# Late storing of the scales, another bank for fillers, and loads of h without pacing in a cross-attention and FFN kernel

## The chip, the cores and the metric

The kernel runs on one core of a Trainium2 chip. The metric is device time in microseconds (us), lower is better. A core has a matrix engine (TensorE, PE in the profile), a vector engine (VectorE, DVE), an activation engine (ScalarE, ACT), a general engine (GpSimd, POOL) and a queue engine (SyncE, SP); each works through its own list of instructions in order and waits on semaphores for the others. DMA transfers are issued here by SP and by POOL, and 16 DMA engines carry them all. PE writes its results to PSUM, 8 banks on chip; SBUF is the large memory on chip, DRAM the one off chip.

## The reference

Input x has 8 x 1024 rows of 512 columns, ctx 8 x 64 rows. In float32:

```python
x = x + xattn(layernorm(x), ctx)      # 16 heads of 64, softmax with a clip at +-11
z = layernorm(x)
# FFN with fake quantisation to 8 bits; scale = sigmoid(clip) * max|.| / 127 over ALL elements
xq = act_fake_quant(z, clip_x)
gate = xq @ weight_fake_quant(w_gate).T    # 512 -> 1408, a scale per output row of the weight
up   = xq @ weight_fake_quant(w_up).T
h = act_fake_quant(silu(gate) * up, clip_down)
out = x + h @ weight_fake_quant(w_down).T  # 1408 -> 512
```

Two maxima over everything cut the work into three: z is quantised only when its last row is known, and h only when the last element of silu(gate)*up is known. These two places are called the first and the second seam.

## The kernel before

The 8192 rows are 64 tiles of 128. **Attention** (0 to 786 us in the profile) runs over the tiles and stores x after attention to DRAM as `x1_d`; in its spare time it also quantises the weights and stores them to DRAM. The scale of each of the 512 rows of w_down ends in the tile `swd` (128 partitions x 4). The kernel writes `swd` to a small DRAM tensor `swd_d` (lines 921 to 923: 512 elements, each its own place in DRAM), so that it can later be loaded broadcast to all partitions as `sdb` (line 1058).

**Gate and up** (791 to 1099 us; lines 993 to 1042) run over 16 groups `g` of 4 tiles (512 rows), and within a group over 11 blocks `i` of 128 features. Per block there are 8 matmuls of 128x512, a Silu on ACT, a product on VectorE, and for every second block a maximum over the pair. A pair of blocks (`j`, 88 in all, 512 KB each in float32) is the unit in which h is kept. PE's results alternate between two buffers `g` (gate) and two buffers `u` (up), one bank each, of the PSUM pool `ps2`. While group g is computed, the rows of group g+1 are made ready: SP loads them from `x1_d` into `xi` (issued at i = 8 two groups ahead; three buffers), VectorE quantises them (`x8`, at i = 2, 3, 5, 6), ACT copies them to bfloat16 (`xb`, one buffer for two tiles, at i = 3, 4, 6, 7), and SP transposes them by DMA into `xT` (`xT<-xb`, two transpositions a group, at i = 4 and i = 7). The first matmul of group g+1 needs both transpositions.

44 pairs (groups 0 to 7) go out to DRAM (`h_d`) as they are made; the other 44 stay on chip: 37 in the pool `hp`, two in PSUM (`pk`), the last five in room of the gate and up weights that is no longer needed.

**The second seam** (lines 1043 to 1058). `keep_clock` issues matmuls whose result nobody reads, so that PE is not idle: 8 before and 5 after the matmul `amh`, through which `all_max` spreads the maximum over all partitions. They write to `kcq`, half of a two-bank buffer `o` of the new PSUM pool `ps3`, which lies where `ps2` was. The matmul `amh` stands behind the first 8 in PE's list.

**The down projection** (1104 to 1259 us; lines 1060 to 1170) takes the pairs in the order `todo`: first the resident ones, then the 44 that are loaded back. `quant_to` quantises pairs some way ahead of PE (ACT to int8, VectorE or every sixth time ACT to bfloat16 `hb`). `load_h` issues the loads `hr<-h_d` on POOL's queue as the count of quantised pairs rises: up to `LD0 + (nld - LD0) * 2 * done / (LDG * 11)` loads, and no more than buffers have come free (`room`). Ahead of each load POOL copies one element of the `hb` of the pair two back into `pace`, so the load goes out no earlier than that pair has been cast. `hp` is shared: from `HBL` pairs before the end the `hb` take its buffers too. `finish` scales the result on VectorE (`wguT<-o,wguT`; the output buffers are also in the old weights' room, hence the name), adds x (`wguT<-wguT,x1r`), stores the output and issues the next load `x1r` on SP's queue (three buffers). For the last group the addition left from the group before is given to POOL (`E=G`). The x of the last group comes by POOL's queue as the last two loads (`hr<-x_d`).

In VectorE's list the casts for later pairs stand behind the `finish` of earlier tiles, and in SP's list each `x1r` behind an output store. All of it is in the order in which the program is written: each call is kept in program order on its engine.

Of the kernel before, what the change touches and what calls it, by code (L numbers as in the profile page):

```python
# [8 lines left out]
F32 = mybir.dt.float32  # L9
F16 = mybir.dt.float16  # L10
BF = mybir.dt.bfloat16
# [3 lines left out]
ALU = mybir.AluOpType  # L15
# [12 lines left out]
KC0 = 12  # L28
KC1 = (2, 7)
KC2 = (8, 5)  # L30
LD0 = 8
LDG = 15
HBL = 33
CAST = 6
XB = 5
# [31 lines left out]
def kernel(  # L67
# [16 lines left out]
    nc = tc.nc  # L84
    V, S, G, T, D = (_InOrder(tc, e) for e in (nc.vector, nc.scalar, nc.gpsimd, nc.tensor, nc.sync))
    P = 128
    NT, DM = x.shape
    NTILE = NT // P
    NGRP = NTILE // 4
# [16 lines left out]
    dram = pool("scratch", space=DRAM)  # L106
# [35 lines left out]
    swd = cst.tile([P, NC], F32, name="swd")  # L142
# [49 lines left out]
    for i in range(4):  # L192
        t = p1.tile([P, DM], F32, tag="x", bufs=XB, name=f"ctxn{i}")
# [13 lines left out]
    for j in range(8):  # L207
        if j == 4:
            for i in range(2):
                c = slice(i * 512, (i + 1) * 512)  # L210
                D.dma_start(out=Wv_s[:, :, c], in_=wkv_v[:, :, 1024:2048][:, :, c])
        r = slice(2 * j % 8, 2 * j % 8 + 2)
        t = p1.tile([P, 2, DM], F32, tag=("e", "ph")[j // 2], bufs=2, name=f"wst{j}") if j < 4 else wof[:, r]
# [435 lines left out]
    FW = {}  # L649
# [78 lines left out]
    def load_x1(g):  # L728
        for t in range(4 * g, 4 * g + 4, 2):
            xi = FW["px"].tile([P, 2, DM], F32, tag="xi", bufs=NXI, name=f"xi{t}")  # L730
            D.dma_start(out=xi, in_=x1_d[t // 2])
            xi_t[t], xi_t[t + 1] = xi[:, 0], xi[:, 1]
# [161 lines left out]
    ps2 = pool("ps2", space=PSUM, es=es2)  # L894
    hp = pool("hp", side="left")

    def keep_clock(q, n, w):

        for _ in range(n):
            T.matmul(q, lhsT=w[:, 0, :], rhs=w, start=True, stop=True)  # L900
# [11 lines left out]
    kcq = ps2.tile([P, 4, P], F32, tag="g", bufs=2, name="kcq").rearrange("p i t -> p (i t)")  # L912
# [4 lines left out]
    keep_clock(kcq, KC1[1], FW["gu"][:, 0, 0])  # L917
    V.reciprocal(gq[:, 1:2], gq[:, 9:10])


    swd_d = dram.tile([DM], F32, tag="swd_d", name="swd_d")
    with nc.allow_non_contiguous_dma(reason="512 scales"):
        D.dma_start(out=swd_d.rearrange("(o p) -> p o", p=P), in_=swd)

    hmx = FW["hmx"]
    x8_t, xb_t = {}, {}

# [56 lines left out]
    x1t = {}  # L984
# [10 lines left out]
    for g in range(NGRP):  # L995
        xT = xTs.pop(g)
        for i in range(NF):
            if g == 0 and i == 0:
                load_x1(1)
            if i == 9 and 0 < g <= NC:  # L1000
                w_trans(5 + g)
            if i == 8 and g + 2 < NGRP:
                load_x1(g + 2)
            k = g * NF + i
            j = k // 2
            h = h_tile(j)[:, k % 2]
            sl = h_tile(JX)[:, 1] if JX - NPK <= j < JX else h
            qs = [ps2.tile([P, 4, P], F32, tag="gu"[w], bufs=2, name=f"q{g}_{i}_{w}") for w in range(2)]
            if k == 0:
                xT = xq_first(qs)  # L1010
            else:
                for w in range(2 if k < NK - 1 else 1):
                    for c in range(NC):
                        T.matmul(qs[w], lhsT=FW["gu"][:, i, w, c, :], rhs=xT[:, :, c, :],
                                 start=(c == 0), stop=(c == NC - 1))
            qs = [q.rearrange("p i t -> p (i t)") for q in qs]
            S.activation(sl, qs[0], AF.Silu, scale=swg[:, 0, i : i + 1])
            if g + 1 < NGRP and i - 1 in XQ:
                xq_b(4 * g + 4 + XQ.index(i - 1))
            if k == NK - 1:  # L1020

                ql = [qs[1], ps2.tile([P, 4, P], F32, tag="g", bufs=2, name="q_half").rearrange("p i t -> p (i t)")]
                for hf in range(2):
                    r = slice(hf * 256, (hf + 1) * 256)
                    for c in range(NC):
                        T.matmul(ql[hf][:, r], lhsT=FW["gu"][:, i, 1, c, :], rhs=xT[:, 2 * hf : 2 * hf + 2, c, :],
                                 start=(c == 0), stop=(c == NC - 1))
                    V.scalar_tensor_tensor(h[:, r], ql[hf][:, r], swg[:, 1, i : i + 1], sl[:, r], ALU.mult, ALU.mult)
                    V.tensor_reduce(hmx[:, j + 2 + hf : j + 3 + hf], h[:, r], AX.X, ALU.max, apply_absolute_value=True)
            else:  # L1030
                V.scalar_tensor_tensor(h, qs[1], swg[:, 1, i : i + 1], sl, ALU.mult, ALU.mult)
                if k >= NK - 4:
                    n = k - NK + NPAIR + 2
                    V.tensor_reduce(hmx[:, n : n + 1], h, AX.X, ALU.max, apply_absolute_value=True)
                elif k % 2:
                    V.tensor_reduce(hmx[:, j : j + 1], h_p[j], AX.XY, ALU.max, apply_absolute_value=True)
            if g + 1 < NGRP and i in XQ:
                xq_a(4 * g + 4 + XQ.index(i))
            if g == NGRP - 1 and i < NXI:
                load_r()  # L1040
            if k % 2 and j < NSP:
                D.dma_start(out=h_d[j], in_=h_p.pop(j))
    es2.close()


    p3 = pool("p3", side="right")
    ps3 = pool("ps3", space=PSUM)
    amh = ps3.tile([P, P], F32, tag="o", bufs=2, name="amh")
    kcq = ps3.tile([P, 2, 512], F32, tag="o", bufs=2, name="kcq")[:, 1]
    keep_clock(kcq, KC2[0], FW["d"][:, :, 0])  # L1050
    V.tensor_reduce(gq[:, 4:5], hmx, AX.X, ALU.max)

    all_max(gq[:, 2:3], gq[:, 4:5], amh,
# [5 lines left out]
    hb_t = {}  # L1059
# [8 lines left out]
    nlo = len(loads)  # L1068
    done = 0
    hbx = None  # L1070
    pace = p3.tile([P, 1], BF, name="pace")

    def load_h(k):

        while loads and nlo - len(loads) < k:
            n = nlo - len(loads)
            j = loads.pop(0)

            G.tensor_copy(pace, hb_t[done - 2][:, 0, 0:1])
            h = w_room(2 * n - 2, 2) if n in (4, 5) else hp.tile([P, 2, 512], F32, tag="h", bufs=NHP, name=f"hr{n}")  # L1080
            if j < 0:
                x1t[-1 - j] = h
                G.dma_start(out=h, in_=x1_d[(-1 - j) // 2])
            else:
                h_p[j] = h
                G.dma_start(out=h, in_=h_d[j])
# [29 lines left out]
            hb_t[done] = hb  # L1116
            done += 1

    def finish(q, t, n, c=slice(0, DM), E=V):

        nonlocal o_n
        o = o_q[o_n % 3][:, t % 2 : t % 2 + n, c]
        V.tensor_tensor(o, q, sdb[:, c].unsqueeze(1).to_broadcast([P, n, c.stop - c.start]), ALU.mult)
        E.tensor_tensor(o, o, x1t[t - t % 2][:, t % 2 : t % 2 + n, c], ALU.add)
        D.dma_start(out=out_v[t // 2][:, t % 2 : t % 2 + n, c], in_=o)
        if (t + n) % 2 == 0 and c.stop == DM:
            o_n += 1
            x1t.pop(t + n - 2)
            load_r()
# [8 lines left out]
    for n, g in enumerate(order):  # L1138
        last = n == NGRP - 1
        q = []  # L1140
        for i in range(4 if last else 2):
            pl, tg = (pk, "hk") if n % 2 and i < 2 else (ps3, "o")
            q.append(pl.tile([P, 2, 4, P], F32, tag=tg, bufs=2, name=f"o{g}_{i}").rearrange("p i c t -> p i (c t)"))
        if last:
            q = [t[:, 0:1] for t in q]
        cuts = (0, NF) if last else (0, 3, 5, 7, 9, 11) if n % 2 else (0, 2, 4, 6, 8, 11)
        for f0, f1 in zip(cuts[:-1], cuts[1:]):
            for i in range(4):

                halves = [slice(0, DM)] if not last or i < 3 else [slice(0, DM // 2), slice(DM // 2, DM)]  # L1150
                for c in halves:
                    o = q[i][:, 0, c] if last else q[i // 2][:, i % 2]
                    if last and c.start:
                        o = pk.tile([P, 2, 512], F32, tag="hk", bufs=NPK, name="o_half")[:, 0, c]
                    for f in range(f0, f1):
                        k = n * NF + f
                        T.matmul(o, lhsT=hb_t[k // 2][:, k % 2, i * P : (i + 1) * P],
                                 rhs=FW["d"][:, c.start // P : c.stop // P, f, :], start=(f == 0), stop=(f == NF - 1))
                    if i == 0:
                        quant_to(-(-(n * NF + f1) // 2) + max(2, n + 8 - NGRP))  # L1160
                        load_h(min(LD0 + (nld - LD0) * 2 * done // (LDG * NF), room()))
                    while ends and (last or i % 2 == 0):
                        finish(*ends.pop(0), E=G if last else V)
                        if not last:
                            break
                    if f1 == NF:
                        if last:
                            finish(o.unsqueeze(1), 4 * g + i, 1, c)
                        elif i % 2:
                            ends.append((q[i // 2], 4 * g + i - 1, 2))  # L1170
# [40 lines left out]
```

## Time and profile before

| what | value |
|---|---|
| time, median of 3 runs | 1267.13 us (1266.77 to 1267.4) |
| the profiled execution's own time | 1267.21 us |
| its span | 1265.1 us |
| PE busy | 1243.3 us, 98% |
| VectorE busy | 1027.1 us, 81% |
| ACT busy | 672.4 us, 53% |
| POOL busy | 336.0 us, 27% |
| loads of h, `hr<-h_d` | 42 of 512 KB, median 7.2 us from issue to landing |
| loads `x1r<-x_d` | 30 of 512 KB, median 6.9 us |
| output stores | 30 of 512 KB, median 5.1 us |
| store `swd_d<-swd` | 1 of 2 KB, 10.4 us |
| transpositions `xT<-xb` | 30, median 3.1 us |

How to read it: the page gives busy times by engine and, in 40 slices of the span, the busy share in tenths, the granted clock of PE (PEclk; 9 stands for 90% or more) and the busy share of the DMA engines. A line of a window gives start and end, the length, the busy time (and number of instructions) of PE, weight loads, DVE, ACT and POOL, the granted clock, the DMA share and GB/s. A line of the timeline gives start, duration, engine, line, operation, output<-inputs, shapes and count, and in brackets how long the engine had been idle before it and who ended that. Nearly all instructions carry line 59, that of the helper that records them, so one goes by the names of the tiles. The duration of a matmul of 128x512 in the rows (0.38 us) contains its way through the array; the next one starts 0.216 us after it.

### The profile page before, as it was taken

How to read it: one execution, taken by the hardware profiler on the slowest of the kernel's cores; microseconds unless marked ns; L12 is line 12 of the kernel's file. 1: busy time of each engine (PE TensorE's matmuls, PEld its weight loads, DVE VectorE, ACT ScalarE, POOL GpSimd, SP SyncE). 2: the span in 40 equal slices, each digit the busy share in tenths (PEclk: the TensorE clock that was granted, in tenths of full speed). 3: DMA queues.
4: the chain of work that ended last, by engine and by line, in shares of the span. 5: the costliest groups of instructions: out<-in, count | busy, mean ns of one | idle time of the engine just before them, and what ended most of it. 6: DMA issues, size and time to landing. Idle time of an engine off the chain costs nothing. (4 is left out here: it accounts for less than half of the span.)

```text
span 1265.1 us, 19838 instructions
## 1 busy us (share of the span) xinstructions
PE 1243.3 (98%) x7395; PEld 570.7 (45%) x7395; DVE 1027.1 (81%) x1663; ACT 672.4 (53%) x855; POOL 336.0 (27%) x411
## 2 busy tenths in 40 slices
PE   8999999999999999999999999999999999999997
PEld 4444444444444444444444445444444444444443
DVE  6998788888888888877777767788888888787787
ACT  6765455555555544445555433455455454467673
POOL 2224433343433443334343342000000000042221
PEclk9999999999999999999999999999999999999999
DMA  9238677787777876668776797778873332299997
GB/s 354 55 70 173 130 153 176 184 173 173 170 179 182 174 158 161 161 165 177 170 171 166 164 191 136 197 242 250 260 214 104 92 100 59 67 330 418 386 346 265
DMA packets 322049, 236.99 MB, mean 187 GB/s; under 512 B 258081, under 2 KB 263713, under 8 KB 321953
## 3 DMA queue, kind: packets, MB, share of 16 engines
q1 hardware_dynamic: 315328, 211.61, 64.7%
q0 software_dynamic: 6624, 24.12, 5.1%
q8 instruction: 58, 0.95, 0.3%
q14 instruction: 39, 0.31, 0.1%
HBM read 112.21 MB, written 60.95 MB: 137 GB/s over the span
## 5 line engine op out<-in xcount | busy, mean ns | idle before, releaser
L59 PE MATMUL sc<-M,lat 128*128 128x512 f16 x1536 | 341.8, 379 | 1.5 <-DMA lat<-lh 1.5
L59 PE MATMUL pv<-N,PT 128*128 128x512 f16 (+1 forms) x1560 | 342.2, 376 | 0.4 <-DVE x L59 0.2
L59 PE MATMUL q<-xT,wguT 128*128 128x512 bf16 x1408 | 304.6, 379 | 2.8 <-DVE h L59 1.6
L59 POOL TENSOR_TENSOR ph<-e,ph 128x1024 f16<-128x1024 f32 x62 | 132.1, 2131 | 401.9 <-ACT ph L59 401.9
L59 PEld LDWEIGHTS <-lat 128*128 128x128 f16 x1536 | 150.0, 98 | 183.2 <-DMA lat<-lh 2.1
L59 PEld LDWEIGHTS <-PT 128*128 128x128 f16 x1560 | 148.3, 98 | 180.1 <-issue 12.4
L59 PEld LDWEIGHTS <-wguT 128*128 128x128 bf16 x1421 | 138.8, 98 | 170.8 <-issue 5.3
L59 ACT ACTIVATE xr<-x,nm 128x512 f32<-128x512 f32 x63 | 45.6, 723 | 237.6 <-DVE nm L59 233.8
L59 ACT ACTIVATE h<-q,swg 128x512 f32<-128x512 f32 x166 | 113.6, 686 | 101.1 <-PE q L59 96.3
L59 DVE SCALAR_TENSOR_TENSOR h<-q,swg,h 128x512 f32<-128x512 f32 x166 | 123.7, 747 | 39.5 <-PE q L59 22.7
L59 PE MATMUL o<-wdT,hb 128*128 128x512 bf16 (+1 forms) x704 | 151.9, 377 | 2.5 <-DVE hb L59 2.1
L59 DVE SCALAR_TENSOR_TENSOR x<-pv,osc,xr 128x512 f32<-128x512 f32 (+1 forms) x65 | 48.2, 742 | 106.6 <-PE pv L59 51.2
L59 POOL COPY pace<-hb 128x1 bf16<-128x1 bf16 x46 | 13.8, 299 | 411.6 <-DVE hb L59 404.7
L59 ACT CAST ph<-e 128x1024 f16<-128x1024 f32 x64 | 66.9, 1045 | 105.2 <-DVE e L59 102.6
L59 PEld LDWEIGHTS <-hb 128*128 128x128 bf16 x715 | 69.3, 98 | 86.6 <-DVE hb L59 6.1
L59 DVE TENSOR_REDUCE hmx<-h 128x1 f32<-128x1024 f32 x83 | 101.3, 1220 | 2.9
L59 POOL TENSOR_TENSOR xr<-xr,bo_b 128x512 f32<-128x512 f32 x64 | 81.7, 1279 | 0.0
L59 DVE SCALAR_TENSOR_TENSOR e<-e,sm 128x1024 f32<-128x1024 f32 x64 | 78.4, 1225 | 2.2
L59 DVE TENSOR_REDUCE sm<-e 128x16 f32<-128x1024 f32 x64 | 78.1, 1220 | 2.2
L59 ACT ACTIVATE e<-sc,esc 128x1024 f32<-128x1024 f32 x64 | 70.9, 1108 | 6.8 <-PE sc L59 3.9
L59 DVE CAST hb<-h 128x1024 bf16<-128x1024 int8 (+2 forms) x77 | 51.3, 678 | 24.0 <-ACT h L59 20.7
L59 ACT CAST xb<-x 128x512 bf16<-128x512 int8 x60 | 36.9, 615 | 43.7 <-DVE x L59 34.7
(173 smaller groups left out, 1269.5 us busy)
## 6 DMA issues: line engine op xcount, KB each, us to landing
h_d<-h SPq DMA_DIRECT2D x44, 512.0 KB, 4.5
hr<-h_d POOLq DMA_DIRECT2D x42, 512.0 KB, 7.2
x<-in_x_dram SPq DMA_DIRECT2D x64, 256.0 KB, 3.1
xr<-in_x_dram SPq DMA_DIRECT2D x64, 256.0 KB, 3.8
x_d<-x SPq DMA_DIRECT2D x64, 256.0 KB, 3.8
xi<-x_d SPq DMA_DIRECT2D x32, 512.0 KB, 4.6
x1r<-x_d SPq DMA_DIRECT2D x30, 512.0 KB, 6.9
out_dram<-wguT SPq DMA_DIRECT2D x30, 512.0 KB, 5.1
```

The costliest lines, as they stand in the source:

```text
L59: r = f(*args, **kwargs)
```

## The change

Five edits, in the order of the program.

1. The store of the scales, `swd_d<-swd`, leaves the first seam. It is issued in group 12 (`NGRP - 4`) ahead of the work of block 7. In SP's list it now stands between the two transpositions for group 13.
2. The first 8 fillers of the second seam write to a buffer `g` of the gate and up pool, taken before that pool is closed (`kcq_d`), and the 5 after `amh` write to the first half of the buffer `o` instead of the second.
3. The copies into `pace` go; a load of h waits only for its buffer's last reader and for the transfer that used its semaphore before it.
4. `LD0` goes from 8 to 10 and `LDG` from 15 to 14, so `load_h` issues more loads at a given count of pairs.
5. `finish` has all additions on VectorE; one instruction moves from POOL to VectorE, behind the scaling of the same tiles.

The lists of PE and ACT keep their instructions in number and order; VectorE's has one addition more near its end, POOL's 48 rows fewer, and SP's one store in another place.

```diff
-LD0 = 8
-LDG = 15
+LD0 = 10
+LDG = 14
...
     V.reciprocal(gq[:, 1:2], gq[:, 9:10])
 
-    swd_d = dram.tile([DM], F32, tag="swd_d", name="swd_d")
-    with nc.allow_non_contiguous_dma(reason="512 scales"):
-        D.dma_start(out=swd_d.rearrange("(o p) -> p o", p=P), in_=swd)
...
             if g == 0 and i == 0:
                 load_x1(1)
+            if g == NGRP - 4 and i == 7:
+                swd_d = dram.tile([DM], F32, tag="swd_d", name="swd_d")
+                with nc.allow_non_contiguous_dma(reason="512 scales"):
+                    D.dma_start(out=swd_d.rearrange("(o p) -> p o", p=P), in_=swd)
...
+    kcq = ps2.tile([P, 4, P], F32, tag="g", bufs=2, name="kcq_d").rearrange("p i t -> p (i t)")
+    keep_clock(kcq, KC2[0], FW["d"][:, :, 0])
     es2.close()
...
     amh = ps3.tile([P, P], F32, tag="o", bufs=2, name="amh")
-    kcq = ps3.tile([P, 2, 512], F32, tag="o", bufs=2, name="kcq")[:, 1]
-    keep_clock(kcq, KC2[0], FW["d"][:, :, 0])
+    kcq = ps3.tile([P, 2, 512], F32, tag="o", bufs=2, name="kcq")[:, 0]
...
-    pace = p3.tile([P, 1], BF, name="pace")
...
             j = loads.pop(0)
-            G.tensor_copy(pace, hb_t[done - 2][:, 0, 0:1])
             h = w_room(2 * n - 2, 2) if n in (4, 5) else hp.tile([P, 2, 512], F32, tag="h", bufs=NHP, name=f"hr{n}")
...
-    def finish(q, t, n, c=slice(0, DM), E=V):
+    def finish(q, t, n, c=slice(0, DM)):
...
-        E.tensor_tensor(o, o, x1t[t - t % 2][:, t % 2 : t % 2 + n, c], ALU.add)
+        V.tensor_tensor(o, o, x1t[t - t % 2][:, t % 2 : t % 2 + n, c], ALU.add)
...
-                        finish(*ends.pop(0), E=G if last else V)
+                        finish(*ends.pop(0))
```

## The prediction

> **What bounds the kernel now.** I read the page's busy table first, then each engine's waits by stretch, then the order of time around the four places that the edits touch. TensorE (PE) is busy 98% of the span at full clock, so an edit counts only through an idle stretch of PE that it closes or opens, or through what runs after PE's last matmul.
>
> ```profile
> PE 1243.3 (98%) x7395; PEld 570.7 (45%) x7395; DVE 1027.1 (81%) x1663; ACT 672.4 (53%) x855; POOL 336.0 (27%) x411
> ...
> PEclk9999999999999999999999999999999999999999
> DMA  9238677787777876668776797778873332299997
> ```
>
> Of gate and up (790 to 1099) the first line below says that the DMA share is only 0.31 where the moved store will land. Of the down projection the second says that the DMA engines are full there while PE never stops.
>
> ```profile
> 1000.00:1040.00 40.00, 40.00 (x188) 18.09 (x185) 34.54 (x44) 20.40 (x33) 0.00 (x0) 1.00 0.31 83
> ...
> 1130.00:1170.00 40.00, 40.00 (x187) 18.19 (x186) 32.70 (x37) 30.36 (x29) 13.19 (x30) 1.00 1.02 412
> ```
>
> At the first seam, in order of time: SP stores the scales (2 KB in 512 pieces) and right behind it issues two loads xi. The store takes 10.4 us to land, the loads 13.4 and 14.0, against a median of 4.6 for all 32 of them. VectorE waits 3.11 us for xi, and PE stops 1.10 and 0.48 us (0.12 more at 808.39).
>
> ```profile
> 787.11 0.43 SPq L59 DMA_DIRECT2D swd_d<-swd  x1
> 787.59 1.04 SPq L59 DMA_DIRECT2D xi<-x_d  x2
> ...
> 801.03 0.55 DVE L59 TENSOR_SCALAR x<-xi,st,r 128x512 int8<-128x512 f32 x1 [3.11 <-DMA xi<-x_d]
> ...
> 802.29 1.89 PE L59 MATMUL q<-xT,wguT 128*128 128x512 bf16 x8 [1.10 <-DVE h L59]
> ...
> 804.66 7.56 PE L59 MATMUL q<-xT,wguT 128*128 128x512 bf16 x33 [0.48 <-DVE h L59]
> ```
>
> At the second seam PE's eight fillers wait 1.36 us for VectorE, and the matmul of the maximum (amh) stands behind them in PE's queue:
>
> ```profile
> 1100.45 1.89 PE L59 MATMUL kcq<-wdT 128*128 128x512 bf16 x8 [1.36 <-DVE wguT L59]
> 1102.18 0.39 PE L59 MATMUL amh<-dgh,ones 128*128 128x128 f32 x2
> ```
>
> At the end the last load of h, held back by its pace copy until 1242.7, lands at 1249.5; ACT, VectorE and PE wait for it in turn. Then VectorE finishes alone, and one of its additions of 0.69 us takes 2.34 while POOL adds beside it:
>
> ```profile
> 1251.55 6.56 PE L59 MATMUL o<-wdT,hb 128*128 128x512 bf16 x35 [1.57 <-DVE hb L59]
> ...
> 1255.10 2.34 POOL L59 TENSOR_TENSOR wguT<-wguT,x1r 128x1024 f32<-128x1024 f32 x1 [6.74 <-DVE wguT L59]
> 1255.65 2.34 DVE L59 TENSOR_TENSOR wguT<-wguT,hr 128x512 f32<-128x512 f32 x1
> ```
>
> **The change part by part.** The sum is made on the profiled execution: 1267.21 us, a span of 1265.1 and 2.1 around it, 0.08 above the median of 1267.13.
>
> *The store leaves the first seam.* The two xi loads then have nothing slow ahead: issued at 787.1, landed by about 793 at 5 us each, wanted at 797.9. The three stops of PE go: -1.7 (1.10+0.48+0.12). No row excludes a little more or less; the ends are -1.1 and -2.0.
>
> *The store comes into group 12.* In SP's queue it stands between that group's two transpositions of x (xT<-xb). The queue row shows both as 1033.26 to 1039.38, 1.23 us each, so SP is free for the store from 1034.5 and gets to the second transposition, which waits for ACT's cast, at 1038.15. That one lands after 3.06 us, at 1041.2. Group 13's first Silu starts at 1043.01, and three matmul steps of 0.216 and one matmul of 0.38 lie ahead of it: PE wants the transposed rows at 1041.97. The slack is 0.8 us. The nearest row for the store is its own: 10.4 us, so 1034.5 to 1044.9, and whatever was issued behind it came late by 9 us. The transposition should then land at 1044.9 plus its own 2.2 (3.06 less about 0.9 from issue to first packet), 1047.1, and PE stops for 5.2. Behind it in SP's queue wait only the two xi loads for group 14, wanted some 10 us later. Ends: 0 (the transposition passes between the pieces), and 6.9 (in the first seam few xi packets ran until 799.2, 1.7 us after the store had landed). I take 5.2, by the row of the same DMA.
>
> *The clock.* A stop of 5.2 us may cost clock too. The nearest row is the end of the span: the last matmul ends at about 1259.3, the clock is still full until 1263.8 and half after that, 4.5 us of idleness.
>
> ```profile
> 1259.50:1263.80 4.30, 0.00 (x0) 0.00 (x0) 2.63 (x6) 0.00 (x0) 0.00 (x0) 1.00 0.70 251
> 1263.90:1265.10 1.20, 0.00 (x0) 0.00 (x0) 0.00 (x0) 0.00 (x0) 0.00 (x0) 0.50 0.00 0
> ```
>
> At the kernel's start the fillers run 3 us at half pace (steps of 0.21 instead of 0.11 us, until 4.3). So a drop costs 1.5 us. One row can't say whether 4.5 us is the least idleness, and 5.2 is close: between 0 and 1.5 I take 0.7. The Trainium skill, TensorE: Matmul & The Clock Gate, section "What's actually happening", lets the clock halve after one idle window of about 3.4 us that runs free of the program; by it alone the drop would be about even odds for this stop, an estimate, and the sum the same within 0.1.
>
> *The first filler in a bank of gate and up.* It takes the buffer whose last reader is the Silu of 1098.26 (0.69 us), done when PE gets there at 1099.1. The eight fillers end near 1100.9 and amh then waits for VectorE's dgh, done at 1101.42, instead of running at 1102.18. The chain through all_max to the first down matmul moves up by 1102.18 less about 1101.70 (LDWEIGHTS 0.2 first): -0.5. Ends 0 and -0.7. The five later fillers only change half a buffer and cost nothing: they stand behind amh, and their bank's readers ended at 1100.3.
>
> *The loads of h without pace.* 46 copies (13.8 us of POOL) go; POOL is idle, so nothing by itself. What changes is when loads start. Each now waits for its buffer's last reader and for the load eight before it, no more. Example: load 28 went out at 1186.7; the reader of its buffer ended near 1158, load 20 landed at 1165. So from 1125 on eight loads are in flight all the time, and all 46 are in by about 1222 instead of 1253. LD0 and LDG allow 10+0.44 per pair done instead of 8+0.44, which fits. Two effects:
>
> At the end nothing waits for h. The last pair's cast, free to follow at 1246.5+1.14+0.69, ends at 1248.3, before PE wants it at 1249.98; the stop of 1.57 goes. VectorE then does two tile pairs (2x2.45), three single tiles (3x1.37) and two halves (2x0.84), bounded at its last step by PE, whose end moves to 1257.7: its last addition ends at 1258.8 instead of 1262.23. That holds the fourth edit, too: the addition on VectorE costs 1.23 and gives back 2.34-0.69 (net -0.4). Together -3.4; ends -0.4 (the load still late) and -3.6.
>
> In the middle the loads compete with SP's queue, which brings x1r and takes out away, 2x0.524 MB per 4.75 us (22 matmul steps of 0.216), 221 GB/s. Today's row for that regime is 1130 to 1170: 412 GB/s, PE without a gap, but x1r landing after 11.1 us (median of the stage 6.9) and one addition already waiting 0.3:
>
> ```profile
>   DMA x1r<-x_d: 0.3, 1
> ...
> DMA to landing us min/median/max: 9.5/11.1/12.9
> ```
>
> Without pace this regime lasts some 52 us longer. POOL's 15 loads there are 197 GB/s, which leaves SP 215 of 221: 2.7% of 52 us, 1.4. By the landings in the trace (one each 2.5 us when deepest) POOL has 210 and SP 202: 8.6%, 4.5. From below, 0, as in the row itself; hb is ready 1 to 3 us ahead of PE there, which absorbs a part. I take +2.0. The Trainium skill, DMA: Bandwidth & Descriptors, section "SWDGE vs HWDGE vs iDMA", has each DMA engine alternate between GpSimd's queue and the others', so the halves would be 206 each: 6.6% or 3.4 us, an estimate, and a sum 1.4 higher.
>
> **Sum.** -1.7 +5.2 +0.7 -0.5 -3.4 +2.0 = +2.3: 1267.2+2.3 = 1269.5.
>
> **The rivals.**
> A, faster: the transposition isn't held by the store. For it: it moves SBUF to SBUF while the store writes DRAM, and 27 of the 30 transpositions xT took 3.0 to 3.1 us in the trace, also beside stores of 512 KB. Against it: xi, too, only wrote SBUF and was held for its whole time. Price: without 5.2+0.7, 1263.6. It decides from a landing before 1045.5: the stop is then under 3.6, too short for the clock, and the sum under zero.
> B, slower: x1r starves in earnest. Three buffers give x1r 14.3 us; it is at 12.9 at worst now. If every addition waits, VectorE's casts behind it come late and PE pays the full 4.5: 1272.0, up to 1273.7 with the longer stop.
> C, the loads do not come earlier: a buffer or the eight-in-flight rule holds them, so only 0.4 of the 3.4 comes, and the +2.0 falls away: 1270.5. Against it stand the semaphores that the changed program's loads wait on: from the twentieth load on they are reached 6 to 37 us before today's issue.
>
> **How the numbers follow.** Forecast 0.50 (own range 1266.5 to 1272.5), A 0.28, B 0.17, C 0.05. About 0.2%, 2.5 us, is what a measurement of this kernel can tell from no change. Faster by more than that: three quarters of A and a little of the forecast, 0.24. Slower: nearly half of the forecast, B, half of C, 0.42. Within: 0.34. Range: A less 0.8 for a milder contention, 1262.8, to short of B's upper end, 1273.2.
>
> **What would show it.** In the profile after: xi landing in about 5 us at the first seam and no wait for it; the second transposition of group 12 landing after 8 to 9 us instead of 3.06 and PE with one gap of about 5 us near 1040; kcq without its wait; no wait for hr at the end, VectorE's last addition about 1 us after PE's last matmul; x1r landing after 11 to 14 us until about 1220 and several gaps of PE of 0.3 to 2 us between 1170 and 1220. The prediction is wrong if that transposition lands in time, or if these gaps are absent.

## The result, and the profile after

The changed kernel takes 1270.73 us (median of 17 runs, 1267.38 to 1273.69) where the kernel before took 1266.94 on the same chip (17 runs, 1265.73 to 1268.51). The ratio is 1.0028, 95% interval 1.0021 to 1.0036: slower by 3.5 us (2.7 to 4.6). The prediction was 1269.5. The profiled execution took 1271.05 us with a span of 1268.9, against 1267.21 and 1265.1 before.

PE is still busy 98%, and in slices the clock still looks full. Of these rows only that of the DMA engines shows something: two slices around the first seam have 5 instead of 7, and the last one 4 instead of 7, as the loads of h are over earlier:

```profile
PE 1246.4 (98%) x7394; PEld 571.7 (45%) x7395; DVE 1026.9 (81%) x1664; ACT 672.9 (53%) x855; POOL 320.8 (25%) x364
...
PEclk9999999999999999999999999999999999999999
DMA  9228577777777876668776795588873232299994
```

A slice is 32 us, too coarse for what happened. Four windows of the changed kernel (the columns are as in the table of before) show two stretches of 3.41 us at half clock, each begun just after a stop of PE, and the DMA engines full from 1130 to 1170 as before:

```profile
1000.00:1040.00 40.00, 40.00 (x188) 18.11 (x186) 34.37 (x45) 20.15 (x32) 0.00 (x0) 1.00 0.33 86
1045.78:1049.19 3.41, 3.41 (x9) 1.20 (x8) 1.97 (x2) 1.07 (x2) 0.00 (x0) 0.50 0.38 155
1130.00:1170.00 40.00, 39.87 (x186) 17.90 (x185) 32.52 (x37) 29.43 (x28) 11.47 (x20) 1.00 1.03 417
1192.55:1195.96 3.41, 3.41 (x9) 1.20 (x8) 2.08 (x3) 3.41 (x4) 0.55 (x1) 0.50 1.02 411
```

*First seam.* In order of time: the two loads xi have nothing slow ahead of them and land 4.3 and 4.9 us after their issue; VectorE takes the first without a wait, and PE runs on there without a stop:

```profile
788.25 0.92 SPq L59 DMA_DIRECT2D xi<-x_d  x2
...
792.68 19.59 PE L59 MATMUL q<-xT,wguT 128*128 128x512 bf16 x90 [0.32 <-DVE xT L59]
...
798.98 0.54 DVE L59 TENSOR_SCALAR x<-xi,st,r 128x512 int8<-128x512 f32 x1
```

*Group 12.* The store went out at 1033.03 and landed 9.4 us later, at 1042.4. The transposition issued behind it at 1036.66 took 7.8 us instead of 3.06 and landed at 1044.4, 2.0 us after the store. PE stood still for 3.90 us, and half clock followed 1.3 us after it had resumed. The last three lines are the store among the DMA issues, the landings of the transpositions between 1030 and 1056, and those of the two between 1030 and 1045 before:

```profile
1033.03 0.57 SPq L59 DMA_DIRECT2D swd_d<-swd  x1
...
1036.66 1.23 SPq L59 DMA_TRANSPOSE xT<-xb  x1
...
1044.48 7.69 PE L59 MATMUL q<-xT,wguT 128*128 128x512 bf16 x27 [3.90 <-DMA xT<-xb]
...
swd_d<-swd SPq DMA_DIRECT2D x1, 2.0 KB, 9.4
...
DMA to landing us min/median/max: 3.1/3.1/7.8
...
DMA to landing us min/median/max: 3.0/3.1/3.1
```

*Second seam.* The first fillers (now `kcq_d`) run without a wait, and amh waits for VectorE instead of standing behind them:

```profile
1103.23 1.89 PE L59 MATMUL kcq_d<-wdT 128*128 128x512 bf16 x8
...
1105.81 0.46 PE L59 MATMUL amh<-dgh,ones 128*128 128x128 f32 x2 [0.69 <-DVE dgh L59]
```

*Middle of the down projection.* At one place x1r is so late that PE pays: VectorE's addition waits 1.64 us for it, the cast behind that addition in VectorE's list is late by as much, and PE waits for the cast.

```profile
1190.01 1.23 DVE L59 TENSOR_TENSOR wguT<-wguT,x1r 128x1024 f32<-128x1024 f32 x1 [1.64 <-DMA x1r<-x_d]
1191.16 0.69 DVE L59 CAST hb<-h 128x1024 bf16<-128x1024 int8 x1
...
1191.90 6.39 PE L59 MATMUL o<-wdT,hb 128*128 128x512 bf16 x21 [2.16 <-DVE hb L59]
```

The view of the tile x1r from 1130 to 1230 has VectorE waiting for it 4.2 us in 4 times (before: 0.3 in one) and these landing times; the last line is the same view of the kernel before:

```profile
  DMA x1r<-x_d: 4.2, 4
...
DMA to landing us min/median/max: 4.1/12.0/13.4
...
DMA to landing us min/median/max: 4.2/7.7/12.9
```

*End.* No wait for h is left, and VectorE's last addition ends 1.03 us after PE's last matmul (1266.02 against 1264.99), where before it was 2.93:

```profile
1263.63 1.36 PE L59 MATMUL o_half<-wdT,hb 128*128 128x256 bf16 x11
...
1265.60 0.42 DVE L59 TENSOR_TENSOR wguT<-wguT,hr 128x256 f32<-128x256 f32 x1
```

Cut at five points of the timeline (first matmul q, first matmul q_half, first matmul o, end of PE's last matmul, end of VectorE's last addition), the profiled executions of this study compare so, in us:

| kernel | first q at | gate and up | second seam | down | to the last addition | span |
|---|---|---|---|---|---|---|
| before | 791.54 | 306.95 | 5.37 | 155.44 | 2.93 | 1265.1 |
| after | 792.68 | 310.05 | 4.84 | 157.42 | 1.03 | 1268.9 |
| store in the last group (e1) | 792.07 | 304.84 | 4.84 | 157.99 | 1.03 | 1263.7 |
| before + edit 1 (e2) | 792.44 | 309.79 | 5.30 | 155.78 | 2.92 | 1269.1 |
| pace back (e3) | 792.77 | 311.12 | 4.84 | 154.80 | 1.09 | 1267.8 |
| before without pace (e4) | 793.51 | 305.82 | 5.37 | 156.09 | 1.42 | 1265.1 |
| before + edits 2 and 5 (e8) | 791.17 | 306.00 | 4.84 | 155.71 | 2.54 | 1263.3 |
| e1 with pace, 8 and 14 (e9) | 792.03 | 304.30 | 4.84 | 153.70 | 1.34 | 1259.1 |
| fillers in the stop (e11) | 791.33 | 308.30 | 4.78 | 156.24 | 1.02 | 1264.5 |
| before, store in the last group (e12) | 792.60 | 304.26 | 5.37 | 157.86 | 1.24 | 1264.2 |

The first column is noise for this question: no edit acts before it, and it varies by 2.3 us. From there on the changed kernel lost 2.6 us: +3.10 in gate and up, -0.53 at the seam, +1.98 in the down projection, -1.90 at the end.

### The profile page after: what moved, and what is told of

The parts are those of the page before. It is cut to its first block, busy times and chain, and to the rows that moved or that the text cites. A ratio compares the mean times of both kernels' runs of the same rounds, so it can differ in the third digit from the quotient of the medians.

```text
span 1268.9 us, 19753 instructions
## 1 busy us (share of the span) xinstructions
PE 1246.4 (98%) x7394; PEld 571.7 (45%) x7395; DVE 1026.9 (81%) x1664; ACT 672.9 (53%) x855; POOL 320.8 (25%) x364
## 5 line engine op out<-in xcount | busy, mean ns | idle before, releaser
L59 POOL DMA_DIRECT2D hr<-h_d x42 | 24.3, 579 | 394.2 <-ACT h L59 363.7
(172 smaller groups left out, 1242.7 us busy)
```

Source lines behind the costliest of these rows:

```text
L59: r = f(*args, **kwargs)
```

## The experiments

Each was run beside the kernel before on the same chip; the ratio is to that.

**Is it the store that stops PE, and does its place matter?** Experiment e1, on the changed kernel:

```diff
-            if g == NGRP - 4 and i == 7:
+            if g == NGRP - 1 and i == 0:
```

> The changed kernel, with the store of the scales at the start of group 15 in place of the middle of group 12; there no transposition is left to come, and the three loads x1r behind it are wanted only some 20 us later. Theory (the store holds the second transposition of group 12): this transposition lands after about 3 us, the stop of 3.90 us at 1044.5 goes, and with it the 3.41 us at half clock behind it, which cost half of that, 1.7 us: 1270.7 - 5.6 = 1265.1 us (1264.0 to 1266.5). The stop of 2.16 us near 1192 stays. First rival (the transposition is late for another reason, ACT's cast or the loads xi): the stop stays and the time is 1270 to 1271. Second rival (the stop goes, but the clock drops at another place): about 1266.8.

Measured 1264.56 us (before 1266.95), ratio 0.9980 (0.9971 to 0.9989): 6.1 us faster than the changed kernel by the two ratios. Gate and up fell by 5.21 us in the profiles, PE has no stop between 922.8 and the second seam, and the stop in the middle stayed (2.74 us, with half clock behind it). The theory holds, both rivals fall. With the store in the last group the changed kernel is faster than before, by 2.5 us; part of that comes from the store's new place itself (e12, below), and what is left for the other four edits, 1.4 us by the two ratios, is within the noise.

Experiment e2 is the kernel before with edit 1 alone:

> The kernel before with the first edit alone: the store goes from the first seam into group 12. Theory: -1.7 (the stops of the first seam) +3.9 (the stop behind the transposition) +1.7 (half clock): 1266.9 + 3.9 = 1270.8 us (1269.5 to 1272); this edit alone would then be about the whole loss, and the other four together near zero. Rival (the loss comes from the loads in the down projection): only the first seam's gain shows, 1265.2 us.

Measured 1272.59 us, ratio 1.0041 (1.0028 to 1.0053), 5.2 us slower: the stop is there (3.74 us, then 3.41 us at half clock), and this one edit costs at least about as much as all five together (the two intervals overlap). Four of its five runs lie above the sum that was expected, and the median above the expected range; the profiled one, the second lowest at 1270.92, is as expected. The rival falls.

Experiment e12 moves the store in the kernel before to the harmless place:

> The kernel before with the store of the scales moved from the first seam to the start of the last group, nothing else changed. Theory: the three stops of the first seam go (1.10 + 0.48 + 0.12, and 0.16 for each restart of PE), nothing comes in their place: 1266.95 - 1.7 to -2.2 = 1265.0 us (1264.6 to 1265.4). Rival (VectorE and ACT are late there for other reasons, as the loads xi land in time but are worked on late): 1266.5 to 1267.

Measured 1265.53 us (before 1266.58), ratio 0.9991 (0.9982 to 1.0000). The theory holds, though the median lies 0.1 us above the expected range. In the profiled execution gate and up gained 2.69 us, more than expected, and 0.73 of it was lost again at the end: the stop for the last load of h was 2.30 us instead of 1.57, with half clock behind it, so that the down projection is 2.42 us longer and the chain behind PE 1.69 shorter:

```profile
1250.64 8.24 PE L59 MATMUL o<-wdT,hb 128*128 128x512 bf16 x35 [2.30 <-DVE hb L59]
```

**What makes the store slow, and how does it hold the transposition?** Experiment e6, on the changed kernel:

```diff
-                    D.dma_start(out=swd_d.rearrange("(o p) -> p o", p=P), in_=swd)
+                    D.dma_start(out=swd_d.rearrange("(p o) -> p o", p=P), in_=swd)
```

> The changed kernel with the store at the same place and in SP's queue, but written in 128 pieces of 16 bytes (each partition's four scales side by side) in place of 512 pieces of 4; the scales are then read back in another order than the columns have, so this run's result is not the reference's, the work is the same. Theory (the price goes by the number of pieces: 9.4 us for 512, of which about 2 us for any small transfer): 2 + 7.4/4, about 3.9 us, landed near 1037, before the second transposition has moved; no stop near 1044, 1265 us. Rival (the price goes by the transfer being a scattered one at all, or by the 128 partitions): 8 to 10 us again and a stop of 3 to 4 us, 1270 to 1271 us.

Measured 1264.98 us (before 1267.19), ratio 0.9983 (0.9973 to 0.9992). The table of DMA issues has the store of the same 2 KB landing in 1.9 us instead of 9.4, and the transpositions back at 3.0 and 3.1:

```profile
swd_d<-swd SPq DMA_DIRECT2D x1, 2.0 KB, 1.9
```

So the price lies in the way the store is cut up and not in the bytes or the 128 partitions. Whether it is the number of the pieces or the size of one, 4 bytes against 16, this run doesn't show, as it changes both; if it is the number, the price falls faster than in proportion, which the estimate of 3.9 us did not have. The Trainium skill, DMA: Bandwidth & Descriptors, section "Anatomy of one DMA — SWDGE (gpsimd) path", gives a DMA on GpSimd's queue about 2.0 us plus its bytes at 436 GB/s. That is 2.0 us for 2 KB, an estimate, but the 512 pieces on that queue took 10.7 (e5, next) and 9.9 us (e13); the 1.9 us of the 128 pieces is near it, on SP's queue.

Experiment e5 gave the store to POOL's queue, at the same place of the program:

```diff
-                    D.dma_start(out=swd_d.rearrange("(o p) -> p o", p=P), in_=swd)
+                    G.dma_start(out=swd_d.rearrange("(o p) -> p o", p=P), in_=swd)
```

> The changed kernel with the store of the scales at the same place of group 12, but issued on POOL's queue in place of SP's; POOL has no other work there. Theory one (order within SP's queue: the transposition's packets are moved at once, but count as landed only behind the store's): the second transposition of group 12 now lands in about 3 us, no stop near 1044, 1265.1 us as with the store in the last group. Theory two (the 512 pieces keep the DMA engines themselves busy, whatever the queue): the transposition lands after 7 to 8 us again, the stop of 3 to 4 us and the half clock behind it stay, 1270 to 1271 us.

Measured 1263.82 us (before 1267.19), ratio 0.9976 (0.9967 to 0.9985), which looks like theory one and is not: POOL, which has nothing to wait for there, issued the store at 788.39, right after the scales and after both loads xi had gone out (from 787.23 on). No transposition was near. The run shows one more harmless place, and nothing on queues. Experiment e13 repeats it with a copy that holds POOL back:

```diff
+                mark = p2.tile([P, 1], F32, name="mark")
+                G.tensor_copy(mark, hmx[:, 68:69])
...
+                    G.dma_start(out=swd_d.rearrange("(o p) -> p o", p=P), in_=swd)
```

> As the run with the store on POOL's queue, but POOL first copies one column of the maxima that is written in group 12, block 5, so that the store cannot go out before about 1034; in the run before this one POOL, which waits for nothing, sent it already at 788. The store's 512 pieces are thus in flight, 1036 to 1045, while the second transposition of group 12 and the two loads xi move on SP's queue. Theory one (order within one queue): the transposition lands after 3.1 us, no stop, 1264.6 us as with the store in the last group, minus or plus 0.8. Theory two (the pieces keep the DMA engines themselves busy): the transposition lands after 6 to 9 us, a stop of 3 to 5 us with half clock, 1270 to 1272 us.

Measured 1270.31 us (before 1266.58), ratio 1.0029 (1.0019 to 1.0040): theory one falls. In order of time in that run, POOL's store (9.9 us to its landing) precedes the second transposition, which SP issues at about 1037.1, on another queue, and which lands only after 8.2 us; PE stops for 4.32, and half clock begins at 1045.27:

```profile
1034.82 0.43 POOL L59 COPY mark<-hmx 128x1 f32<-128x1 f32 x1 [245.13 <-DVE hmx L59]
1035.20 1.01 POOL L59 DMA_DIRECT2D swd_d<-swd  x1
...
1045.32 7.00 PE L59 MATMUL q<-xT,wguT 128*128 128x512 bf16 x24 [4.32 <-DMA xT<-xb]
```

What is shared is thus behind the queues. Theory two said "busy", and that isn't shown either: from 1035 to 1045 the profile has the DMA engines at a share of only 0.26 in both runs, so they stand more than they work while the pieces are outstanding. The packets themselves tell more. In the changed kernel no packet of the store is recorded after 1034.6, though it landed at 1042.4, and the packets of the transposition ran from 1037.8 to 1039.3, as this row of the window from 1037 to 1040 shows (40 slices of 0.075 us):

```profile
DMA  0000000000039999999999999999310000000000
```

In e6 they ran until 1039.3 too, and the transposition had landed at 1039.8; here it landed at 1044.4, and in e13, with packets until 1039.7, at 1045.3. So by these records the transposition's data moved in time, and what came late was the report that it is complete. That is theory one's picture of packets that move at once and count later, but not as the order within one queue. The two loads xi behind it were slow in their packets too: 25 of their 256 are recorded from 1040 to 1044, where e6 has all 256 from 1039.2 to 1042.6. What the report waits for these runs can't tell.

**What did the clock cost?** Experiment e11, on the changed kernel, ahead of group 13:

```diff
+        if g == NGRP - 3:
+            kcq = ps2.tile([P, 4, P], F32, tag="g", bufs=2, name="kcq_s").rearrange("p i t -> p (i t)")
+            keep_clock(kcq, 16, FW["gu"][:, 0, 0])
```

> The changed kernel with 16 filler matmuls, 3.5 us whose result nobody reads, ahead of group 13, where PE stands still for 3.9 us behind the second transposition; they need only the weights and a buffer that is free by then. The stop's length for the work does not change, but PE is not idle in it. Theory (the stop costs its own 3.9 us and, through the clock, 1.7 us more): the first half-clock stretch goes, the transposition still lands 7 to 8 us after its issue, 1270.7 - 1.7 = 1269.0 us (1268 to 1269.8). Rival (the half clock costs nothing, PE would wait for ACT and VectorE after the stop anyhow): 1270.7. Second rival (the fillers end after the transposition has landed and delay the work): 1270 to 1271.

Measured 1267.52 us, ratio 1.0007 (0.9998 to 1.0016). The transposition lands as late as in the changed kernel (7.8 us), PE does useless work until 0.48 us before that, and no half clock follows:

```profile
1038.98 3.62 PE L59 MATMUL kcq_s<-wguT 128*128 128x512 bf16 x15
1043.07 9.24 PE L59 MATMUL q<-xT,wguT 128*128 128x512 bf16 x42 [0.48 <-DMA xT<-xb]
```

Gate and up is shorter by 1.75 us in the profiles, as expected; by the ratios the gain is 2.7 us (0.0021 of 1267), the intervals allowing 0.6 to 4.8, and the median lies half a us under the expected range. The rivals fall. The mean granted clock over the runs is 0.9968 in the changed kernel and 0.9992 here; 0.0024 of 1269 us is 3.0 us, in which the half clock behind the stop in the middle counts too, as it comes in some runs and not in others.

**Why does PE stop in the middle, and which edit brings it?** Experiment e3 puts the copies into `pace` back into the changed kernel, e4 takes them from the kernel before:

```diff
             j = loads.pop(0)
+            G.tensor_copy(pace, hb_t[done - 2][:, 0, 0:1])
```

> The changed kernel with the copies into pace ahead of the loads of h put back, LD0 = 10 and LDG = 14 kept. Theory (loads that run ahead of the casts starve x1r): x1r lands as in the kernel before (median 11.1 us in the same stretch, VectorE's waits for it near 0.3 us in all instead of 4.2), the stop of 2.16 us near 1192 and the 1.7 us of half clock behind it go; the last load is issued at 81.5 pairs done instead of 87, five pairs or some 8.7 us earlier than in the kernel before, lands near 1245 and not 1249.5, so the stop of 1.57 us at the end does not come back: 1270.7 - 3.9 = 1266.8 us (1265.5 to 1268.5). Rival (the larger counts LD0 and LDG starve x1r, with or without pace): the waits for x1r and the stop stay, 1270 to 1271.

Measured 1267.74 us (before 1266.95), ratio 1.0005 (0.9996 to 1.0013): 2.9 us faster than the changed kernel by the ratios, 3.9 expected. The stop at the end stayed away, the one in the middle shrank to 1.23 us without half clock but did not go: x1r still lands after 10.3 us (median; 7.7 before) and VectorE waits for it 2.4 us. So the larger counts starve x1r by themselves, though less than the two edits together.

> The kernel before without the copies into pace, LD0 = 8 and LDG = 15 kept, nothing else changed. Theory (without pace the loads start as buffers come free, whatever the counts): the stop of 1.57 us at the end goes, one of about 2.2 us comes near 1190, and 1.7 us of half clock in some executions: 1266.9 - 1.6 + 2.2 + 1.0 = 1268.5 us (1267.3 to 1270). Rival (the counts hold the loads, pace adds nothing): 1266.9, the stop of 1.57 stays. Second rival (only the gain at the end shows, no starving): 1265.3.

Measured 1266.02 us, ratio 0.9994 (0.9985 to 1.0002); 1268.5 was expected, and none of the three cases was right. Its stops in the middle are those of the theory, 2.13 us at 1188.99 and 0.53 at 1208.69, and VectorE waits 4.4 us for x1r, as much as with both edits; so the missing pace does it whatever the counts. But the stop at the end went, so that the down projection is only 0.65 us longer than before, the chain behind PE shrank by 1.51, and no half clock followed the stop in the profiled execution. (The 1.13 us that gate and up is shorter are no work of this edit, which acts later: the first of the stops at the first seam was 0.32 us in this execution and 1.10 in that of before.) Without pace the trade alone is even, or a little better than even.

Experiment e10, on e1, lightens SP's queue and changes no instruction of PE, ACT or VectorE:

```diff
-        D.dma_start(out=out_v[t // 2][:, t % 2 : t % 2 + n, c], in_=o)
+        D.dma_start(out=out_v[t // 2][:, t % 2 : t % 2 + 1, c], in_=o[:, 0:1])
```

> The changed kernel with the store of the scales in the last group (so without the stop near 1044), and with each output store of two tiles cut to the first of the two: half of the output of all but the last group is left out, and SP's queue carries 0.524 + 0.262 MB per 4.75 us, 165 GB/s in place of 221. No instruction of PE, ACT or VectorE changes. Theory (the stop of 2 to 2.7 us near 1187 comes from bandwidth: POOL's eight loads in flight leave SP's queue less than x1r and the output need): x1r lands after 8 us or less in the stretch, VectorE's waits for it (4.3 us in 4) and PE's stop go: 1264.6 - 2.4 - about 1 for half clock in some executions = 1261.3 us (1260.5 to 1262). Rival (the stop comes from the order of casts and additions in VectorE's list around that place, not from the transfers): the stop stays at 2 us or more, 1264 to 1265 us.

Measured 1261.47 us (before 1266.58), ratio 0.9959 (0.9944 to 0.9974), 2.7 us under e1, whose interval it just touches; the profile is clearer. PE has no stop of 0.6 us or more after amh, and VectorE no wait for x1r, whose landings are now:

```profile
DMA to landing us min/median/max: 3.6/8.2/11.2
```

The order of VectorE's list is the same, so the rival falls: with fewer bytes on SP's queue the stop goes, so it comes from bandwidth. That POOL's loads take it shows in e9 below, where SP's bytes are all there, the loads of h are held back, and the stop is gone as well.

**The small edits.** Experiment e8 is the kernel before with edits 2 and 5 (fillers in another bank, all additions on VectorE):

> The kernel before with two small edits alone: the first eight fillers of the second seam in a bank of gate and up, and all additions on VectorE. Expected by the terms of the prediction: -0.5 (amh 0.5 us earlier) and -0.4 (VectorE's addition 0.69 instead of 2.34, one addition more): 1266.95 - 0.9 = 1266.0 us (1265.6 to 1266.4), the stop of 1.57 us near 1251 still there. Rival (the addition on VectorE lengthens the chain behind PE's last matmul by its 1.2 us): 1266.4 + 0.8 = 1267.2.

Measured 1266.06 us (before 1267.19), ratio 0.9986 (0.9978 to 0.9995), 1.8 us (0.6 to 2.8). The seam fell from 5.37 to 4.84 and the chain behind PE from 2.93 to 2.54. Both terms hold; the rest is within the interval, and 0.95 us by which gate and up is shorter in the profiled execution is no work of these edits (the first of the stops at the first seam was 0.27 us).

**A version that beats both.** Experiment e9 is the changed kernel with the store in the last group, the pace back, and other counts:

```diff
-LD0 = 10
+LD0 = 8
 LDG = 14
...
-            if g == NGRP - 4 and i == 7:
+            if g == NGRP - 1 and i == 0:
...
+            G.tensor_copy(pace, hb_t[done - 2][:, 0, 0:1])
```

> The changed kernel with the store in the last group, the copies into pace put back, and LD0 = 8, LDG = 14 (8 loads ahead as in the kernel before, but a steeper rise, so that the last load goes out at 81 pairs done instead of 87). Theory: in the middle as in the kernel before (stops of PE under 0.5 us, no half clock), at the end no stop: 1264.6 - 2.74 - 0.16 - half of 1.7 = 1260.8 us (1260 to 1262). First rival (the stop of 1.6 us at the end comes back): 1262.4. Second rival (as with LD0 = 10 and pace, a stop of about 1.2 us near 1187 stays): 1262.1.

Measured 1261.55 us (before 1267.19), ratio 0.9960 (0.9946 to 0.9973): 5.1 us faster than before, some 8.6 faster than the changed kernel. PE's order of time in the down projection is one row from 1103.42 to its last matmuls, so neither rival came:

```profile
1103.42 150.25 PE L59 MATMUL o<-wdT,hb 128*128 128x512 bf16 x696 [0.34 <-DVE hb L59]
1253.51 1.36 PE L59 MATMUL o_half<-wdT,hb 128*128 128x256 bf16 x11
```

x1r lands there after a median of 9.6 us, at worst 13.3, and VectorE waits for it 2.0 us in three times; as PE has no gap for it, the casts were far enough ahead to absorb that.

## Why the prediction was right, and where its steps were not

The sign, the two places of loss and the total held: +2.3 by the sum, +2.6 in the profiled executions from the first matmul q on, 3.5 by the ratio. The terms:

- *The store leaves the first seam, -1.7.* Too small. Gate and up without any of these stops takes 304.26 to 304.39 us (e12, e9, e10), so before it lost 2.6 to 2.7. The step counted only the idle gaps. A gap is measured from the end of a matmul's row of 0.38 us, while the next one would have started 0.216 after its start, so every restart costs 0.16 us more: 0.5 for three. The other 0.4 to 0.5 is not pinned down; the stop of 0.77 near 924, which no edit touches and which is 0.4 to 0.8 in the others, is a part of it. That the first stop was 0.32 in e4 and 1.10 before says how far one execution carries here; by e12 the whole edit is worth 2.0 us in the profile, after what the end took back, and 1.1 by the ratio (0 to 2.3).
- *The store comes into group 12, +5.2.* Right in kind: the transposition landed 2.0 us after the store (2.2 in the step). Mis-sized: the step's own numbers give 5.1 rather than 5.2, and the stop was 3.90, or 4.06 with its restart, as the store took 9.4 us here and 10.4 at the first seam. The reason given in rival A against it, that what runs behind the store is held whatever it moves, holds even on another queue (e13). Rival A was to decide from a landing before 1045.5 or a stop under 3.6. The landing was at 1044.4, but PE wanted the rows at 1040.4 and not at 1042.0, having no stops at the first seam, so the transposition was held all the same and the stop was 0.3 us over the limit; but the rival's reason, that such a stop is too short for the clock, was wrong, as the next step shows.
- *The clock, +0.7.* This step failed. It took 1.5 us at even odds from one row of 4.5 us of idleness. Half clock came with the stop behind this transposition in all four profiled executions that had it unfilled (after, e2, e3, e13); it lasts 3.41 us (6.83 in e3) and costs half of that, 1.71, and it followed the stop of 2.16 us in the middle as well, which the step did not ask about. By e11 the first of them is worth 1.75 in the profile.
- *The first filler in a bank of gate and up, -0.5.* 5.37 became 4.84. Right.
- *The end, -3.4.* The stop of 1.57 is gone and the chain behind PE is 1.90 shorter: -3.5. Right, the last addition about 1 us behind PE included.
- *The middle, +2.0.* Right in mechanism (e10) and in the landings of x1r (12.0, at worst 13.4, where 11 to 14 was said), but the loss was one stop of 2.16 and not several of 0.3 to 2: with its restart and its half clock 4.0 us, near the end of 4.5 that was kept for the range. The term came from a deficit of bandwidth spread over 52 us, and the profile shows it gathered in one place; why in this one is open.

So four terms were off, by 0.9 and 1.1 us to one side and by 1.0 and 2.0 to the other, and most of that cancelled: the signs and the places were understood, but that the total came within 1.2 us is partly luck. Rival B came in part, as 4 additions in 20 waited. Rival C fell: the last load of h went out at 1215.1 instead of 1242.7.

## What to carry to other kernels

Look at what stands behind a small scattered store, not at its bytes: 512 pieces of 4 bytes took 9 to 11 us to land and held what came after them until then, on their own queue and on another one; at a place with nothing urgent behind it, or as 128 pieces of 16 bytes, the store made PE stop nowhere. A pace on prefetches that looks like a needless wait can be what leaves another queue its bandwidth; bringing its last loads forward by a steeper count was worth 2.5 us more than removing it (e9 against e1, two intervals that just touch). Price a stop of the matrix engine with its restart and with the clock, and ask in which stretch of 3.41 us it falls.

## What the runs showed of the hardware that was not expected

*The clock looks at fixed stretches.* In each of the eight profiled executions, of fourteen, in which half clock begins more than once, the beginnings lie whole multiples of 3.413 us apart. With each of the fourteen cut into these stretches, from 20 us to PE's last matmul, every stretch of full clock in which PE had been idle for 2.03 us or more was followed by half clock in the next one (12 of them, 2.03 to 3.41 us idle), and none with 2.02 us or less (the nearest: 2.02 and 1.90). One stretch at half clock with 1.37 us of idleness was followed by another (e3). So a stop of 2.16 us costs 1.7 more if it falls into one stretch, and nothing more if the border cuts it; a stop of 2.21 in e5 and one of 2.24 in e11 were cut so. This would also explain, though only one run of each kernel has a trace, why the changed kernel's runs spread over 6.3 us and those of before over 2.8: the lowest granted clock of its runs, 0.994, goes with 1272.68 and 1273.69 us, and 0.999 to 1.000 with 1267.38 to 1269.25. The Trainium skill, TensorE: Matmul & The Clock Gate, section "What's actually happening", has the free-running stretch of 3413 ns, which agrees; it names an idle window as the condition, where here 2.03 us out of 3.41 was enough.

*Pieces outstanding hold transfers of other queues while the DMA engines look idle.* In e13 the transposition's report came 5.6 us after its last packet and 0.2 us after the store's. There the two loads xi behind the held transposition took 10.6 us (median) and the DMA engines' share was 0.26 from 1035 to 1045. The skill's page DMA: Bandwidth & Descriptors, section "Back-pressure in remote DMA", says that stalled writes stall an engine's other queues too, of transfers between cores; e13 is in keeping with that for a store to DRAM, but doesn't prove the cause.
